# Handing dt·u·B from TensorE to VectorE by PSUM banks in a four-layer scan kernel

## The chip, the cores and the metric

The kernel runs on one core of a Trainium2 chip, as one program for all four layers. The metric is the device time of one execution in microseconds. Engines are called by the profile's names: PE (TensorE, the matmuls), PEld (its weight loads), DVE (VectorE), ACT (ScalarE), POOL (GpSimd), SP (the queue that issues most DMAs).

## What is computed

A picture of 4 x 64 x 64 positions and 192 channels goes through four layers, each with a group norm ahead of it and a residual sum behind it. Layers 0 and 3 scan every image in four directions (rows, columns, and both backwards); layer 1 does the same with sequences of only 64 positions, one per line; layer 2 is a Toeplitz product and has no scan. The change concerns the selective scan that layers 0, 1 and 3 share. Cut to its core, for every channel and each of 16 states:

```python
def step(h, inp):
    u_l, dt_l, Bl, Cl = inp
    dA = jnp.exp(dt_l[..., None] * A[None])
    h = dA * h + (dt_l * u_l)[..., None] * Bl[:, :, None, :]
    y = jnp.sum(h * Cl[:, :, None, :], axis=-1)
    return (h, y)
```

In layers 0 and 3 the state `h` runs through all 4096 positions of an image; in layer 1 it starts at zero on every line of 64.

## The kernel before

**Jobs and units.** The sequence is cut into chunks of 512 positions (`T`). One chunk in one direction is a *job*: 128 jobs in each of layers 0, 1 and 3. A job is cut into *units*: 64 channels times 4 of the 16 states. The 128 partitions hold the 64 channels twice (`q` = 0, 1), each half with two states along the free dimension, so a unit is a tile of 128 x 1024. Layers 0 and 1 have 384 inner channels and 24 units per job, layer 3 has 192 and 12.

**One unit, engine by engine.**
- PE makes `b` = dt·u·B in PSUM (`feed`, line 378): the transposed dt·u of 64 channels is the loaded weight, a diagonal matrix of B values (`diag`) is what streams. A unit takes 4 position blocks of 128 (`k`) times 2 halves (`q`), 8 products of 256 columns. An fp32 product shows as two MATMUL records, so a fill of `b` is 16 records.
- ACT makes dA = exp(dt·A) by two instructions of 512 elements (line 401), into one of three SBUF tiles.
- DVE runs the recurrence (`scan`): in layers 0 and 3 one scan of 512 per state, with a carry from the chunk before (line 418); in layer 1 a single scan of 1024 (line 411), since dA is zero at the start of each line.
- POOL multiplies by C (line 422), and PE sums the two partition halves and the states into `y` (`collect`, line 447, four records of 512 columns per unit).

**Direct units.** In part of the units (pair `p` = 3; one of two channel groups in layer 0, both in layers 1 and 3: 3 of 24, 6 of 24, 3 of 12 units per job) PE has no part in `b`. POOL makes it in SBUF (`spread`, line 351), and dA goes into the PSUM tile that `b` would have had.

**Layout of `b`.** The PSUM tile is 128 x 1024 fp32, two banks of 512, and there are two such tiles (pool `b`, 2 buffers). In layers 0 and 3 the states alternate element by element (`(l n)`): block `k` fills 256 neighbouring elements, blocks 0 and 1 the first bank, 2 and 3 the second, and either state's scan reads every second element of both banks. In layer 1 the tile is `(h n l)`: the first half of the positions with both states is the first bank, the second half the second.

**What sets the order.** The whole program is unrolled. `run_jobs` walks over the units; at unit i it issues `feed` of unit i+2, `scan` of unit i, `spread` of unit i+3, `collect` of a finished pair, and then the preparatory steps that are due there by hand-set offsets (`when`: projections, softplus in `finish`, line 271, the product dt·u, line 278, transposes `turn`, line 285, step sizes, line 259) and the loads that `plan` places. Each engine works through its own instructions in that order. Waits are placed by the framework from the regions that instructions read and write. dt·u is made by DVE in layer 0 and 3 (line 278) and by POOL in layer 1.

**Around the scans.** Each image of layers 0 and 3 also has an input stage (norm, projection, convolution) and an output stage; they are not touched.

Of the kernel before, what the change touches and what calls it, by code (L numbers as in the profile page):

```python
# [9 lines left out]
ALU = mybir.AluOpType  # L10
# [9 lines left out]
T = 512  # L20
# [3 lines left out]
NB = T // 128  # L24
# [12 lines left out]
class Kernel:  # L37
# [316 lines left out]
    def feed(self, job, t, p, c, pools):  # L354

        nc = self.nc
        w, rev, g = job["w"], job["rev"], 2 * t + c
        lines = job["carry"] is None
        direct = c in job["direct"].get(p, ())
        wide = pools["b"].tile([128, 2 * T], F32, name="b")  # L360
        if direct:
            b = job["bs"].pop((t, p, c))
        else:
            b = wide
        for k in range(0 if direct else NB):
            for q in range(2):
                half = b[q * 64 : (q + 1) * 64, :]
                if lines:
                    to = half.rearrange("p (h n l) -> p h n l", h=2, n=2)
                    off = k % 2 * 128  # L370
                    to = to[:, k // 2, :, off : off + 128]
                else:
                    to = half[:, k * 256 : (k + 1) * 256].rearrange("p (l n) -> p n l", n=2)
                if isinstance(job["dtuT"], dict):
                    dtu = job["dtuT"][t][:, k, c * 64 : (c + 1) * 64]
                else:
                    dtu = job["dtuT"][:, k, g * 64 : (g + 1) * 64]
                nc.tensor.matmul(  # L378
                    to, dtu, job["diag"][p][:, k, 2 * q : 2 * q + 2, :],
                    start=True, stop=True,  # L380
                )
        delta = job["both"][g]
        if lines:
            if job.get("begin"):
                job.pop("begin")()
            if direct:
                dA = wide
                at = HW - 1 if rev else 0
                nc.scalar.copy(dA[:, at::HW], job["zero"])
            else:  # L390
                self.turns_dA += 1
                dA = job["dA"][self.turns_dA % len(job["dA"])]
            inner = slice(0, HW - 1) if rev else slice(1, HW)
            of = delta.rearrange("p (h a b) -> p h a b", h=2, b=HW)[:, :, :, inner]
            to = dA.rearrange("p (h n a b) -> p h n a b", h=2, n=2, b=HW)[:, :, :, :, inner]
            to = [to[:, :, n] for n in range(2)]
        else:
            of, dA = delta, wide if direct else pools["work"].tile([128, 2 * T], F32, name="dA", bufs=3)
            to = [dA[:, n * T : (n + 1) * T] for n in range(2)]
        for n in range(2):  # L400
            nc.scalar.activation(to[n], of, AF.Exp, scale=w["A"][:, g, 2 * p + n : 2 * p + n + 1])  # L401
        job["fed"][t, p, c] = b, dA, direct

    def scan(self, job, t, p, c, pools):
        nc = self.nc
        rev, carry, g = job["rev"], job["carry"], 2 * t + c
        way = slice(None, None, -1) if rev else slice(None)
        b, dA, direct = job["fed"].pop((t, p, c))
        h = pools["work"].tile([128, 2 * T], F32, name="h", bufs=7 if carry is None else 4)
        if carry is None:  # L410
            nc.vector.tensor_tensor_scan(h[:, way], dA[:, way], b[:, way], 0.0, ALU.mult, ALU.add)  # L411
        else:
            by_n = b.rearrange("p (n l) -> p n l" if direct else "p (l n) -> p n l", n=2)
            dA = dA.rearrange("p (n l) -> p n l", n=2)
            hn = h.rearrange("p (n l) -> p n l", n=2)
            for n in range(2):
                start = 0.0 if job["first"] else carry[g, p][:, n : n + 1]
                nc.vector.tensor_tensor_scan(  # L418
                    hn[:, n, way], dA[:, n, way], by_n[:, n, way], start, ALU.mult, ALU.add
                )  # L420
        hc = h if carry is None else pools["work"].tile([128, 2 * T], F32, name="hc", bufs=5)
        nc.gpsimd.tensor_mul(hc, h, job["cbc"][p])  # L422
        job["done"][t, p, c] = hc
        if carry is None:
            return None

        def after():
            nc.scalar.copy(carry[g, p], hn[:, :, 0 if rev else T - 1])

        return after  # L430
# [799 lines left out]
```

## Time and profile before

| what | value |
|---|---|
| median of 3 runs | 30885.05 us (30880.78 to 30885.68) |
| the profiled execution: its own time | 30865.86 us |
| its span, first to last instruction | 30864.0 us, mean granted PE clock 0.961 |
| busy share of the span: PE, DVE, ACT, POOL | 87%, 72%, 75%, 74% |
| layer 0, scans of one image (32 jobs) | about 2285 us, four times |
| layer 1, all scans (128 jobs) | 10905 us |
| layer 3, scans of one image (32 jobs) | about 1234 us, four times |

The three scan stages were found from the first and the last of POOL's products by C. Divided by their jobs they give 71.4, 85.2 and 38.6 us per job. The shares of the page are means over stages with different limits, so the three stages have to be read apart. A group line of the page reads: line of the kernel, engine, operation, tile written and tiles read, shape, count; then busy us and mean ns of one; then the idle time just before these instructions and what ended it. A timeline line reads: start and length in us, engine, line, operation, count of merged instructions, and in brackets the idle time before it and what ended it. Matmul records overlap: their spacing from start to start is what PE needs, not their length.

### The profile page before, as it was taken

To read this page: it belongs to the slowest core of one execution; us is meant where nothing else is said; L and a number is where in the kernel's file an instruction comes from. 1 tells how busy PE (TensorE), PEld (TensorE's weight loads), DVE (VectorE), ACT (ScalarE), POOL (GpSimd) and SP (SyncE) were. 2 spreads that over 40 slices of the span, in tenths; PEclk is the share of its full clock that TensorE was granted. 3 is DMA by queue.
4 is the path that set the end of the run, shared out by engine and by line. 5 is a ranking of instruction groups with operands and counts; after the bars stand their busy time and mean duration, and the time that the engine had idled before them with its cause. 6 is when DMAs were issued, how large, how long until landed. Compare 5 with 4: busy or idle time off the path is not lost. (4 is left out here: it accounts for less than half of the span.)

```text
span 30864.0 us, 503255 instructions
## 1 busy us (share of the span) xinstructions
PE 26878.4 (87%) x189464; PEld 15827.7 (51%) x189464; DVE 22327.6 (72%) x16587; ACT 23000.6 (75%) x50177; POOL 22890.6 (74%) x9831
## 2 busy tenths in 40 slices
PE   8998998999899688888888888888588988888888
PEld 5664665666466444444444444444355444444444
DVE  7887888788788777777777777777423267777777
ACT  7885886788588588888888888888232278788888
POOL 7885885888588499989998999999100077777777
PEclk9999999999999899999999999999788999999999
DMA  3334333433433533333333333333533345545454
GB/s 109 100 99 117 101 98 104 112 100 99 119 101 97 142 99 97 97 100 101 101 104 97 98 97 99 102 101 102 131 78 76 104 131 131 132 130 134 128 135 128
DMA packets 1652695, 3342.38 MB, mean 108 GB/s; under 512 B 396725, under 2 KB 453494, under 8 KB 1634646
## 3 DMA queue, kind: packets, MB, share of 16 engines
q1 hardware_dynamic: 1541718, 3142.34, 38.1%
q10 hardware_dynamic: 108544, 167.85, 1.6%
q8 instruction: 1497, 24.53, 0.4%
q14 instruction: 936, 7.67, 0.1%
HBM read 2149.81 MB, written 656.08 MB: 91 GB/s over the span
## 5 line engine op out<-in xcount | busy, mean ns | idle before, releaser
L378 PE MATMUL b<-diag,dtuT 128*64 128x256 f32 x98304 | 12607.9, 386 | 1732.9 <-DVE h L411 917.9
L422 POOL TENSOR_TENSOR hc<-h,c 128x1024 f32<-128x1024 f32 x4608 | 10943.4, 2395 | 1515.0 <-DVE h L418 1158.3
L378 PEld LDWEIGHTS b<-diag,dtuT 128*64 128x64 f32 x98304 | 8214.9, 138 | 6212.3 <-DVE h L411 1903.3
L401 ACT ACTIVATE dA<-both,A 128x512 f32<-128x512 f32 (+1 forms) x12288 | 8267.7, 711 | 2124.3 <-DVE h L411 1472.0
L418 DVE TENSOR_TENSOR_SCAN h<-dA,carry,b 128x512 f32<-128x512 f32 x6720 | 8169.8, 1263 | 1367.8 <-PE b L378 861.4
L422 POOL TENSOR_TENSOR h<-h,c 128x1024 f32<-128x1024 f32 x3072 | 7219.1, 2374 | 1049.2 <-DVE h L411 880.3
L332 ACT ACTIVATE diag<-ident,bt 128x128 f32<-128x128 f32 x20480 | 6570.6, 391 | 92.2 <-issue 91.4
L447 PE MATMUL y<-hc,fold 128*64 128x512 f32 x18432 | 5783.3, 599 | 386.1 <-POOL hc L422 384.4
L411 DVE TENSOR_TENSOR_SCAN h<-dA,b 128x1024 f32<-128x1024 f32 x2304 | 5202.8, 2274 | 1147.3 <-ACT dA L401 798.4
L351 POOL TENSOR_TENSOR bs<-dtu,bc 128x1024 f32<-128x1024 f32 x1536 | 3639.4, 2369 | 158.5 <-DMA c<-bc_dram 72.8
L447 PE MATMUL y<-h,fold 128*64 128x512 f32 x12288 | 3259.6, 593 | 10.2 <-POOL h L422 10.2
L501 POOL MEMSET pad<- 128x13068 f32 (+1 forms) x8 | 73.4, 9172 | 3968.3 <-DMA inw<-in_L_in_w 2997.7
L411 DVE TENSOR_TENSOR_SCAN h<-b,bs 128x1024 f32<-128x1024 f32 x768 | 1758.9, 2290 | 1413.6 <-ACT b L401 1102.8
L447 PEld LDWEIGHTS y<-hc,fold 128*64 128x64 f32 x18432 | 1924.0, 138 | 1550.1 <-POOL hc L422 813.1
L401 ACT ACTIVATE b<-both,A 128x504 f32<-128x504 f32 (+1 forms) x3072 | 2076.2, 676 | 376.4 <-DVE h L418 328.3
L418 DVE TENSOR_TENSOR_SCAN h<-b,carry,bs 128x512 f32<-128x512 f32 x1344 | 1639.2, 1260 | 220.9 <-issue 170.4
L237 PEld LDWEIGHTS dtu_ps<-ident,dtu 128*64 128x64 f32 (+1 forms) x16384 | 1183.2, 141 | 497.6 <-issue 375.9
L447 PEld LDWEIGHTS y<-h,fold 128*64 128x64 f32 x12288 | 1005.0, 137 | 795.2 <-issue 444.9
L418 DVE TENSOR_TENSOR_SCAN h<-dA,b 128x512 f32<-128x512 f32 x960 | 1112.8, 1205 | 352.8 <-PE b L378 191.3
L401 ACT ACT_TABLE_LOAD x1019 | 1307.4, 1283 | 11.8
L237 PE MATMUL dtu_ps<-ident,dtu 128*64 128x128 f32 (+1 forms) x16384 | 1272.7, 273 | 45.9 <-DVE dtu L278 41.5
L827 DVE SCALAR_TENSOR_TENSOR u<-in_ps,conv_w,u 128x504 f32<-128x504 f32 (+2 forms) x1152 | 831.6, 722 | 411.7 <-ACT u L822 402.6
(157 smaller groups left out, 24601.4 us busy)
## 6 DMA issues: line engine op xcount, KB each, us to landing
c<-bc_dram SPq DMA_DIRECT2D x3072, 256.0 KB, 4.1
both<-delta SPq DMA_DIRECT2D x2048, 128.0 KB, 2.7
bc<-bc_dram SPq DMA_DIRECT2D x768, 256.0 KB, 4.2
both<-delta_dram SPq DMA_DIRECT2D x1536, 128.0 KB, 3.7
dtu<-dtu_dram SPq DMA_DIRECT2D x1536, 128.0 KB, 2.7
dtu<-dtu SPq DMA_DIRECT2D x1280, 128.0 KB, 2.5
L_y<-out ACTq DMA_DIRECT2D x512, 256.0 KB, 3.0
u<-L_u SPq DMA_DIRECT2D x160, 768.0 KB, 5.4
```

The costliest lines, as they stand in the source:

```text
L237: nc.tensor.matmul(to[half * 64 : (half + 1) * 64], of[:, half * 64 : (half + 1) * 64], self.ident[:p, :p], start=True, stop=True,)
L332: nc.scalar.activation(to, self.ident, AF.Copy, scale=of)
L351: self.nc.gpsimd.tensor_mul(by(b), dtu, by(job["bbc"][p]))
L378: nc.tensor.matmul(to, dtu, job["diag"][p][:, k, 2 * q : 2 * q + 2, :], start=True, stop=True,)
L401: nc.scalar.activation(to[n], of, AF.Exp, scale=w["A"][:, g, 2 * p + n : 2 * p + n + 1])
L411: nc.vector.tensor_tensor_scan(h[:, way], dA[:, way], b[:, way], 0.0, ALU.mult, ALU.add)
L418: nc.vector.tensor_tensor_scan(hn[:, n, way], dA[:, n, way], by_n[:, n, way], start, ALU.mult, ALU.add)
L422: nc.gpsimd.tensor_mul(hc, h, job["cbc"][p])
L447: nc.tensor.matmul(y[c * 64 : (c + 1) * 64, :], self.fold, of, start=first == 0 and n == 0, stop=last == LAST and n == 1)
L501: nc.gpsimd.memset(pad, 0.0)
L827: nc.vector.scalar_tensor_tensor(u[:, :, to], ps[:, :, of], tap(3 - j), u[:, :, to], ALU.mult, ALU.add)
```

## The change

In layers 0 and 3 each state gets one bank of the PSUM tile: the products are cut from 256 to 128 columns, all of state 0 first (blocks 0 to 3, both halves), then all of state 1. A fill is then 16 products, 32 records, in place of 8 and 16, and the scan of a state reads one bank, element after element. In layer 1 the products stay as they are, but backward directions make blocks 2 and 3 before 0 and 1, and the scan of 1024 is cut into two scans of 512, each over one bank, both with the start value 0.0; in backward directions the upper one runs first.

```diff
+        turns = []
+        if lines and not direct:
+            turns = [(k, slice(0, 2)) for k in ((2, 3, 0, 1) if rev else range(NB))]
+        elif not direct:
+            turns = [(k, slice(n, n + 1)) for n in range(2) for k in range(NB)]
+        for k, n in turns:
-        for k in range(0 if direct else NB):
             for q in range(2):
                 half = b[q * 64 : (q + 1) * 64, :]
                 if lines:
...
                 else:
-                    to = half[:, k * 256 : (k + 1) * 256].rearrange("p (l n) -> p n l", n=2)
+                    off = n.start * T + k * 128
+                    to = half[:, off : off + 128]
...
-                nc.tensor.matmul(
-                    to, dtu, job["diag"][p][:, k, 2 * q : 2 * q + 2, :],
-                    start=True, stop=True,
-                )
+                of = job["diag"][p][:, k, 2 * q + n.start : 2 * q + n.stop, :]
+                if not lines:
+                    of = of[:, 0, :]
+                nc.tensor.matmul(to, dtu, of, start=True, stop=True)
...
         if carry is None:
-            nc.vector.tensor_tensor_scan(h[:, way], dA[:, way], b[:, way], 0.0, ALU.mult, ALU.add)
+            for at in (T, 0) if rev else (0, T):
+                one = slice(at, at + T)
+                nc.vector.tensor_tensor_scan(
+                    h[:, one][:, way], dA[:, one][:, way], b[:, one][:, way], 0.0, ALU.mult, ALU.add
+                )
         else:
-            by_n = b.rearrange("p (n l) -> p n l" if direct else "p (l n) -> p n l", n=2)
+            by_n = b.rearrange("p (n l) -> p n l", n=2)
```

`lines` and `carry is None` mean layer 1; `direct` units have no products. Nothing else changes.

## The prediction

> **What bounds the kernel now.** I read the page's groups first, then the busy time of each engine in the scan stages (image 0 of layer 0, all of layer 1, image 0 of layer 3), then the timeline of single jobs.
>
> ```profile
> L378 PE MATMUL b<-diag,dtuT 128*64 128x256 f32 x98304 | 12607.9, 386 | 1732.9 <-DVE h L411 917.9
> L418 DVE TENSOR_TENSOR_SCAN h<-dA,carry,b 128x512 f32<-128x512 f32 x6720 | 8169.8, 1263 | 1367.8 <-PE b L378 861.4
> L411 DVE TENSOR_TENSOR_SCAN h<-dA,b 128x1024 f32<-128x1024 f32 x2304 | 5202.8, 2274 | 1147.3 <-ACT dA L401 798.4
> ```
>
> ```profile
> core 0: us, PE busy (x) PEld busy (x) DVE busy (x) ACT busy (x) POOL busy (x), PEclk, DMA share, GB/s
> 190.00:2475.00 2285.00, 2135.26 (x16612) 1487.15 (x16608) 1955.75 (x1612) 1897.95 (x4702) 2021.31 (x863) 0.97 0.38 97
> 10811.00:21716.00 10905.00, 9711.19 (x69924) 5058.93 (x69922) 7956.07 (x4717) 9104.84 (x16955) 9856.90 (x4358) 1.00 0.35 99
> 24875.00:26109.00 1234.00, 1085.58 (x8120) 651.97 (x8120) 987.65 (x828) 1169.91 (x2996) 1149.70 (x480) 1.00 0.52 135
> ```
>
> Three limits: in layer 0 PE is busy 93% of the stage, in layer 1 POOL 90%, in layer 3 ACT 95%. In layer 0 DVE often waits for a fill of `b`:
>
> ```profile
> DVE h L418 <- PE b L378: 223.0, 251, 2.2
> ```
>
> That is 7.0 us in each of the 32 jobs. One job, PE and then ACT:
>
> ```profile
> 1502.50 1.93 PE L378 MATMUL b<-diag,dtuT 128*64 128x256 f32 x16
> 1504.22 1.06 PE L447 MATMUL y<-hc,fold 128*64 128x512 f32 x4
> 1505.08 1.93 PE L378 MATMUL b<-diag,dtuT 128*64 128x256 f32 x16
> ...
> 1516.01 3.68 PE L378 MATMUL b<-diag,dtuT 128*64 128x256 f32 x16 [3.87 <-DVE h L418]
> ```
>
> ```profile
> 1526.60 1.34 ACT L401 ACTIVATE dA<-both,A 128x512 f32<-128x512 f32 x2 [2.38 <-DVE h L418]
> 1529.21 0.72 ACT L401 ACTIVATE dA<-both,A 128x512 f32<-128x512 f32 x1 [1.19 <-DVE h L418]
> ```
>
> PE runs without a hole except once a job: DVE waits for softplus and makes dt·u (1508.33, 2.82 us), both PSUM tiles stay full, PE stands 3.87 us and restarts cold. So a job of layer 0 is a loop: PE fills (1516 to 1529), DVE's scans end, ACT gets its dA tiles back (1529.21) and is then nearly gapless until the next job's softplus, dt·u, two units of scans, PE.
>
> [...] a scan that reads both banks starts only after a fill's last record, 0.14 us behind it. [...] with every second element written a fill goes from first to last start in 1.93 - 0.38 = 1.55 us, in layer 1 with runs of 128 in 1.95 - 0.38 = 1.57. I book no gain for the contiguous write. [...]
>
> **The change part by part.**
>
> *Products of 128 columns.* The fill takes 1504.22 - 1502.50 = 1.72 us, 16 records at 108 ns[...]. The transposes have the shape that comes (64 weights, 128 columns):
>
> ```profile
> 2023.26 0.71 PE L237 MATMUL dtu_ps<-ident,dtu 128*64 128x128 f32 x9
> 22326.89 21.44 PE L1080 MATMUL yt_ps<-xt,mat 64*64 64x64 f32 x384 [0.57 <-ACT xt L1073]
> ```
>
> (0.71 - 0.27) / 8 = 55 ns from start to start, with a weight load for each; layer 2 holds (21.44 - 0.28) / 383 = 55.2 ns over 384 records. So 32 records take 1.74 to 1.77 us; I take +0.03 us a fill (ends +0.01 and +0.05).
>
> *The handoff.* A wait goes by the region read, a tile's reuse by the whole tile:
>
> ```profile
> 2032.21 2.45 DVE L418 TENSOR_TENSOR_SCAN h<-dA,carry,b 128x512 f32<-128x512 f32 x2 [1.01 <-PE b L378]
> 2032.33 0.72 ACT L401 ACTIVATE dA<-both,A 128x512 f32<-128x512 f32 x1
> ```
>
> The first scan starts before ACT has begun the second half of its dA, so it will also start on bank 0 while PE fills bank 1. But ACT at 1526.60 starts when both scans of the tile's last user are over (1524.11 + 2.45), though the first had freed its half 1.2 us before. So PE doesn't get a tile back sooner; only DVE gets it earlier, by half a fill, 0.86 us, plus 0.11 because the last record lasts 273 ns in place of 386. The first scan (1.20 us) covers the rest of the fill, so the pair ends 0.97 us earlier wherever DVE was waiting for PE, as at 1526.73.
>
> *Layer 0 on its chain.* ACT's wait ending at 1529.21 shortens by 0.97. Behind it ACT has 0.1 and 0.8 us of slack left until softplus; I carry 0.9 us to dt·u and to PE's restart. The three fills between restart and 1529 cost 3 x 0.03 = 0.1. In jobs where softplus hangs on PE more directly, 21 fills cost 0.6, of which a PE wait on DVE of 0.5 (at 2136.83) absorbs most. Net -0.85 us a job, x 128 = **-109 us**; ends -0.6 and -1.1: -77 to -140. Hidden: DVE's other 6 us of waits per job. They are PE's own pace (a unit with a transpose needs 1.73 + 0.86 + 0.87 = 3.46 us of PE), and an earlier start of a scan doesn't speed that.
>
> *Layer 1.* Two scans for one:
>
> ```profile
> 26411.32 4.55 DVE L418 TENSOR_TENSOR_SCAN h<-dA,b 128x512 f32<-128x512 f32 x4 [9.51 <-DMA dtu<-dtu]
> 14999.81 4.46 DVE L411 TENSOR_TENSOR_SCAN h<-dA,b 128x1024 f32<-128x1024 f32 x2
> ```
>
> 4.55 against 4.46 us: +0.05 us a unit, on all 3072 (154 us of DVE time, mostly hidden: DVE is busy 73%). A job's chain goes POOL's `bs` (15032.0), two scans, ACT, one scan, ACT gapless, one scan, ACT, one scan (15082.30), POOL: five scans, +0.25 us, x 128 = **+32 us** (0 to +70). The earlier start wins nothing there: these scans wait for ACT or POOL, and each exp writes both banks of a direct tile. ACT, queued behind a scan for its dA tile, is in the five.
>
> *Layer 3.* ACT is the limit; its waits (0.93 and 0.68 us a job at 27328.16 and 27329.51) hang on a projection behind PE's fill, not on the handoff: 2 x 0.03 x 128 = **+6 us** (-30 to +20).
>
> Sum: -109 + 32 + 6 = -71 us on 30865.86 gives 30795; the median lies 19 us above the profiled run: **30814 us**.
>
> **Rivals.**
> - *PE pays for the split (slower).* If a weight load (138 ns) no longer hides behind a product half as long, each record costs more. Layer 0 is PE-bound, so 21 fills a job pay: at 58 ns a record a fill is 1.86 us, 21 x 0.13 - 1.4 = +1.3 us a job, +166, and with +38 from the other layers 31090. It decides from about 55.7 ns: 21 x 0.052 us equals the gain less those 38 us. For it: that is only 0.5 ns above the 384-record run, and PEld is already busy 65% in layer 0. Against it: both bursts hold 55 ns with a load for every record.
> - *The handoff isn't on the path.* If ACT's own queue paces softplus, layer 0 stays, the rest costs 38: 30923. That the scan waited for the whole tile after all gives the same time. Against it: the 1.19 us wait at 1529.21.
> - *The hole shrinks too.* PE's stop is 3.87 to 4.48 us. The cold fill spreads its starts over 2.8 us in place of 1.6, and the transposes behind it lose as much. If half of the 128 jobs stay warm, 64 x 2.4 = 154 us more: 30660. Against it: both ends of the hole move together.
>
> **How the numbers follow.** Forecast 0.55, slower PE 0.18, no path 0.14, warm restart 0.13. About 0.2%, 62 us, is what a measurement of this kernel can tell from no change. The forecast's own ends are 30740 to 30880; I put 0.35 of its 0.55 below 30823 and 0.20 within. With the warm restart faster is 0.48; same 0.20 + 0.08 = 0.28; slower 0.18 + 0.06 = 0.24. The range 30620 to 31000 leaves out the dearer half of the first rival and a little below.
>
> **What would show it.** Right: L378 records in layer 0 at 54 to 56 ns from start to start; DVE's wait for `b` there well below 223 us an image; its scan starting under half a fill after the first record; 70.5 us a job in layer 0, 85.5 in layer 1, 38.6 in layer 3. Wrong: records above 56 ns, a PE fill that starts before both scans of the tile's last user end, or a layer 3 that moves by over 0.3 us a job.

## The result, and the profile after

The changed kernel takes 31288.92 us (median of 4 runs, 31284.16 to 31294.73), the kernel before, in the same session, 30885.36 (30880.78 to 30887.13): ratio 1.0132, 95% interval 1.012 to 1.0144. It is 404 us slower, outside the stated range of 30620 to 31000. The profiled execution spans 31292.9 us, 428.9 more than that of before.

The groups of the page; the lines of the kernel have moved (378 is now 387, 401 is 407, 411 is 419, 418 is 428, 422 is 432, 447 is 457), and move again in the kernels of the experiments:

```profile
L387 PE MATMUL b<-diag,dtuT 128*64 128x128 f32 (+1 forms) x159744 | 12804.9, 304 | 2043.6 <-DVE h L419 1124.9
...
L428 DVE TENSOR_TENSOR_SCAN h<-dA,carry,b 128x512 f32<-128x512 f32 x6720 | 8179.3, 1264 | 1406.2 <-PE b L387 951.4
...
L419 DVE TENSOR_TENSOR_SCAN h<-dA,b 128x512 f32<-128x512 f32 x4608 | 5351.4, 1204 | 1285.2 <-ACT dA L407 846.1
```

PE has more records (159744 against 98304) for nearly the same busy time (12804.9 us against 12607.9), DVE's scans of layers 0 and 3 cost what they did (1264 ns against 1263), and layer 1's cost more: 149 us in the units that PE fills (5351.4 against 5202.8), 47 in the direct ones (1805.9 against 1758.9). And DVE's idle time ended by PE's `b` has grown from 861.4 to 951.4, where the forecast wanted it to shrink. The busy time of the engines in image 0 of layer 0, in layer 1 and in image 0 of layer 3 (columns as in the prediction's table):

```profile
190.00:2480.00 2290.00, 2118.60 (x27116) 1660.59 (x27114) 1940.78 (x1598) 1898.81 (x4689) 2001.43 (x854) 0.97 0.37 98
10850.00:21950.00 11100.00, 9892.98 (x69966) 5882.37 (x69968) 8070.04 (x7786) 9169.48 (x17011) 9829.55 (x4348) 0.98 0.34 98
25152.00:26426.00 1274.00, 1104.84 (x12696) 797.99 (x12696) 990.73 (x829) 1176.11 (x2997) 1149.89 (x480) 0.98 0.49 131
```

No engine does much more than before (the largest rise is PE's in layer 1, 9892.98 us against 9711.19); all three stages are longer. From POOL's first to its last product by C, layer 0 takes 2310.5 us an image (2282.9 before, means of four), layer 1 11062.8 (10904.6), layer 3 1273.4 (1233.9): +110, +158 and +158 us, together 427 of the 429 us between the two traces.

**The handoff isn't split.** DVE's waits for a fill in image 0 of layer 0 rose from 223.0 us (us in total, number of waits, longest):

```profile
DVE h L428 <- PE b L387: 259.2, 367, 3.8
```

PE and DVE in one job of that image:

```profile
1520.95 1.92 PE L387 MATMUL b<-diag,dtuT 128*64 128x128 f32 x32
1522.70 1.03 PE L457 MATMUL y<-hc,fold 128*64 128x512 f32 x4
...
1523.02 2.45 DVE L428 TENSOR_TENSOR_SCAN h<-dA,carry,b 128x512 f32<-128x512 f32 x2 [1.02 <-PE b L387]
```

The fill's last record ends at 1520.95 + 1.92 = 1522.87, and the pair of scans starts at 1523.02: 0.15 us behind the whole tile, as before, and not behind the half that the first scan reads. It is so throughout: of the 2688 fills of layer 0, the 2304 of layer 1 and the 1152 of layer 3 none has a scan that starts before the fill's last record has ended.

**Where the time goes.** POOL takes each unit's product in a fixed order, so the mean idle time ahead of the product of unit 0, 1, 2 ... of a job shows where a job got longer. The means here and below leave out the first and the last job of an image (of 32 jobs in layer 1). Most of the 24 (12) units moved by under 0.06 us; those that moved most, mean us a job:

| layer, unit | before | after |
|---|---|---|
| 0, unit 5 (direct) | 0.02 | 0.62 |
| 1, unit 17 | 0.00 | 1.05 |
| 1, unit 18 | 1.26 | 0.52 |
| 1, unit 20 | 0.00 | 0.21 |
| 1, unit 21 (direct) | 0.00 | 0.54 |
| 3, unit 5 (direct) | 0.00 | 0.90 |
| 3, unit 9 (direct) | 1.58 | 2.24 |

**What stands there in the traces.** The engines don't issue their instructions as the program text has them: the framework lays out each engine's order, and after the change it laid it out anew. Of the 50177 places in ScalarE's sequence 9002 hold another operation than before, of GpSimd's 9831 none. In layer 0 TensorE's sequence changed as well, VectorE's did not; in layers 1 and 3 VectorE's changed too, in layer 3 in 28 places. In layer 0, ACT around unit 5, before:

```profile
483.68 0.58 ACT L616 COPY out<-y 128x512 f32<-128x512 f32 x1
...
484.15 0.73 ACT L401 ACTIVATE dA<-both,A 128x512 f32<-128x512 f32 x1
...
484.78 0.68 ACT L401 ACTIVATE b<-both,A 128x512 f32<-128x512 f32 x1
...
485.39 0.71 ACT L401 ACTIVATE dA<-both,A 128x512 f32<-128x512 f32 x1
...
486.00 0.68 ACT L401 ACTIVATE b<-both,A 128x512 f32<-128x512 f32 x1
...
486.78 2.46 DVE L418 TENSOR_TENSOR_SCAN h<-b,carry,bs 128x512 f32<-128x512 f32 x2 [0.20 <-ACT b L401]
```

and after, in the same job:

```profile
489.02 1.35 ACT L407 ACTIVATE dA<-both,A 128x512 f32<-128x512 f32 x2
...
490.26 0.59 ACT L626 COPY out<-y 128x512 f32<-128x512 f32 x1
...
490.73 0.43 ACT L332 ACTIVATE diag<-ident,bt 128x128 f32<-128x128 f32 x1
...
491.27 0.69 ACT L407 ACTIVATE b<-both,A 128x512 f32<-128x512 f32 x1
...
491.98 0.72 ACT L407 ACTIVATE dA<-both,A 128x512 f32<-128x512 f32 x1
...
492.61 0.67 ACT L407 ACTIVATE b<-both,A 128x512 f32<-128x512 f32 x1
...
493.38 2.46 DVE L428 TENSOR_TENSOR_SCAN h<-b,carry,bs 128x512 f32<-128x512 f32 x2 [1.34 <-ACT b L407]
```

The direct unit's two exps (written to a `b` tile) now stand behind both of another unit's dA, a copy and a diagonal; DVE waits 1.34 us for the second in place of 0.20. In layer 3's backward jobs, PE and DVE before:

```profile
26895.96 1.03 PE L447 MATMUL y<-hc,fold 128*64 128x512 f32 x4
26896.82 0.59 PE L625 MATMUL fold_ps<-out,fold 128*64 128x512 f32 x1
...
26899.26 0.66 DVE L614 TENSOR_TENSOR out<-fold_ps,earlier 64x512 f32<-64x512 f32 x1
```

and after:

```profile
27215.99 1.03 PE L457 MATMUL y<-hc,fold 128*64 128x512 f32 x4
27220.32 1.08 PE L457 MATMUL y<-hc,fold 128*64 128x512 f32 x4 [3.29 <-POOL hc L432]
27221.23 0.59 PE L635 MATMUL fold_ps<-out,fold 128*64 128x512 f32 x1
...
27222.29 0.68 DVE L624 TENSOR_TENSOR out<-fold_ps,earlier 64x512 f32<-64x512 f32 x1 [3.52 <-PE fold_ps L635]
27222.90 2.44 DVE L428 TENSOR_TENSOR_SCAN h<-b,carry,bs 128x512 f32<-128x512 f32 x2
```

The fold product (it adds the two partition halves of a finished `out`), for which everything was there, now stands on PE behind a `y` product that waits 3.29 us for POOL. DVE stands in front of `out` for 3.52 us, and the scan that POOL needs next is queued behind it. In layer 1, DVE after:

```profile
11836.71 1.21 DVE L419 TENSOR_TENSOR_SCAN h<-dA,b 128x512 f32<-128x512 f32 x1
11837.84 0.71 DVE L837 SCALAR_TENSOR_TENSOR u<-in_ps,conv_w,u 128x496 f32<-128x496 f32 x1
11838.46 1.21 DVE L419 TENSOR_TENSOR_SCAN h<-dA,b 128x512 f32<-128x512 f32 x1
11839.59 0.70 DVE L837 SCALAR_TENSOR_TENSOR u<-in_ps,conv_w,u 128x488 f32<-128x488 f32 x1
```

With two half scans to a unit, an operation of the convolution (a *tap*, line 837) can be set between the halves, and POOL, which needs both, waits for it (0.88 us ahead of its product at 11839.82). This is so in 378 units, three a job.

### The profile page after: what moved, and what is told of

The parts are those of the page before. It is cut to its first block, busy times and chain, and to the rows that moved or that the text cites. A ratio compares the mean times of both kernels' runs of the same rounds, so it can differ in the third digit from the quotient of the medians.

```text
span 31292.9 us, 634272 instructions
## 1 busy us (share of the span) xinstructions
PE 27122.6 (87%) x250904; PEld 17972.8 (57%) x250904; DVE 22478.4 (72%) x19659; ACT 23095.9 (74%) x50177; POOL 22899.0 (73%) x9831
## 5 line engine op out<-in xcount | busy, mean ns | idle before, releaser
L387 PE MATMUL b<-diag,dtuT 128*64 128x128 f32 (+1 forms) x159744 | 12804.9, 304 | 2043.6 <-DVE h L419 1124.9
L387 PEld LDWEIGHTS b<-diag,dtuT 128*64 128x64 f32 x159744 | 10529.2, 139 | 5249.9 <-issue 2708.9
L428 DVE TENSOR_TENSOR_SCAN h<-dA,carry,b 128x512 f32<-128x512 f32 x6720 | 8179.3, 1264 | 1406.2 <-PE b L387 951.4
L419 DVE TENSOR_TENSOR_SCAN h<-dA,b 128x512 f32<-128x512 f32 x4608 | 5351.4, 1204 | 1285.2 <-ACT dA L407 846.1
L457 PE MATMUL y<-hc,fold 128*64 128x512 f32 x18432 | 5431.2, 602 | 510.2 <-POOL hc L432 510.0
L457 PE MATMUL y<-h,fold 128*64 128x512 f32 x12288 | 3560.8, 609 | 8.9 <-POOL h L432 8.9
L419 DVE TENSOR_TENSOR_SCAN h<-b,bs 128x512 f32<-128x512 f32 x1536 | 1805.9, 1211 | 1269.3 <-POOL h L432 515.5
L457 PEld LDWEIGHTS y<-hc,fold 128*64 128x64 f32 x18432 | 1556.0, 138 | 1351.8 <-POOL hc L432 924.3
L457 PEld LDWEIGHTS y<-h,fold 128*64 128x64 f32 x12288 | 1180.7, 142 | 716.5 <-issue 490.3
L428 DVE TENSOR_TENSOR_SCAN h<-dA,b 128x512 f32<-128x512 f32 x960 | 1111.5, 1205 | 374.9 <-PE b L387 204.5
```

The costliest lines, as they stand in the source:

```text
L387: nc.tensor.matmul(to, dtu, of, start=True, stop=True)
L419: nc.vector.tensor_tensor_scan(h[:, one][:, way], dA[:, one][:, way], b[:, one][:, way], 0.0, ALU.mult, ALU.add)
L428: nc.vector.tensor_tensor_scan(hn[:, n, way], dA[:, n, way], by_n[:, n, way], start, ALU.mult, ALU.add)
L457: nc.tensor.matmul(y[c * 64 : (c + 1) * 64, :], self.fold, of, start=first == 0 and n == 0, stop=last == LAST and n == 1)
```

## The experiments

Kernel 1 is the kernel of experiment 1, and so on. Theory O: the loss is the new order of instructions. Theory P: it is the operations themselves, twice the products in layers 0 and 3 and twice the scans in layer 1. To tell them apart, an engine's order is *tied*: the program is laid out once in the version whose order is wanted, and in the version that runs the instructions of each engine are chained in that order. The chain fixes the order of issue and is declared without a wait (`NoSync`); where a fill or scan has another number of instructions, the group stands where the other's stood. In the traces of kernels 1 to 3 the sequences of ScalarE, VectorE and GpSimd agree with those wanted in every place (a unit's two half scans counted as one).

```diff
+    nc = make(NEW, BANKS, make(LIKE, LIKE_BANKS))
...
+            tc.add_manual_dep(i, last[e].name, free, reason="order")
```

**1. New operations, old order** (NEW: layers 0, 1, 3; LIKE: the kernel before; all engines).

> All operations are those of the changed kernel; only the order in which each engine (TensorE, VectorE, ScalarE, GpSimd, SyncE) issues them is tied to that of the kernel before (a fill of 32 products stands where the fill of 16 stood, the two half scans of layer 1 stand together where the one scan stood). Theory O (the loss is the new order of instructions that the scheduler chose when the operations changed): layer 0 back to about 2283 us an image, layer 3 to 1234, layer 1 to 10905 to 10940 (five scans a job on the chain by 0.05 us: at most +32), in all 30,870 to 30,940, ratio 0.9995 to 1.002. Theory P (the loss is the operations themselves: twice the products, twice the scans, more semaphore signals): about 31,290 as the changed kernel, ratio 1.013.

Measured: 30931.22 us, ratio 1.0021 (1.0013 to 1.0029). Layer 0 2288.7 us an image, layer 1 10944.0, layer 3 1234.5. The idle time of units 5 in layers 0 and 3 is gone (0.02 and 0.00 us), and layer 1's extra 39 us are in units 18 and 0, ahead of which POOL already waited. This is what theory O said: the operations alone make 64 us, against the 30867.61 that the kernel before took in the same session.

**2. Old operations, new order** (NEW: none; LIKE: the changed kernel).

> The reverse: all operations are those of the kernel before, 256-column products and one scan a unit in layer 1; each engine issues them in the order of the changed kernel (a fill or a scan stands where the last part of its group stood). Theory O: the loss comes without the change, layer 0 about 2310 us an image, layer 3 about 1273, layer 1 11,020 to 11,070, in all 31,220 to 31,300, ratio 1.011 to 1.0135. Theory P: 30,885 within 0.2%, ratio 1.000.

Measured: 30850.61 us, ratio 0.9995 (0.9986 to 1.0004): the total fits theory P, and the layers show that this is chance. Layer 3 takes 1272.5 us an image, all of the changed kernel's loss without one changed operation. Layer 0 takes 2287.2, only +4. Layer 1 takes 10711.7, which is 193 *less* than before. So O holds in layer 3, and in layer 1 the new order is good as long as a scan is one instruction. In layer 0 the two don't add: order alone +17 us over four images, operations alone +23, both +110. The 0.6 us ahead of unit 5 come with the order (0.59 here), but with the old operations the job wins 0.41 back ahead of unit 15 (0.29 against 0.70), with the new ones nothing (0.74).

**3. A real handoff by banks, old order.** As 1, and in layers 0 and 3 each bank is a tile of its own.

```diff
+            wide = [pools["b"].tile([128, T], F32, name="b", bufs=4) for n in range(2)]
...
+                    to = b[n.start][rows, k * 128 : (k + 1) * 128]
```

> As the first kernel of this call (new operations in the old order), and in layers 0 and 3 the two PSUM banks of a unit are two tiles of their own instead of one tile of two banks, so the first scan waits for the 16 records of its own bank only, and a bank is filled again as soon as its own scan is over. This makes the handoff that the forecast assumed. If the forecast's layer 0 step holds once the handoff is really split: layer 0 by 20 to 35 us an image below the first kernel (2250 to 2263), layer 3 within 3 us of it, in all 30,760 to 30,840. If the handoff is not on the path (the second rival): layer 0 within 8 us an image of the first kernel, in all within 30 us of it.

Measured: 30581.15 us, ratio 0.9907 (0.9892 to 0.9922), more than expected. Layer 0 takes 2186.9 us an image, 102 less than kernel 1; layer 3 1248.7, 14 more. DVE's waits for `b` in image 0 of layer 0:

```profile
DVE h L446 <- PE b L401: 150.0, 258, 1.8
```

It was 237.4 in kernel 1. One fill, on the timeline:

```profile
1608.95 1.63 PE L401 MATMUL b<-diag,dtuT 128*64 128x128 f32 x26
1610.37 0.59 PE L475 MATMUL y<-hc,fold 128*64 128x512 f32 x1
1610.42 0.49 PE L401 MATMUL b<-diag,dtuT 128*64 128x128 f32 x3
...
1610.18 3.88 DVE L446 TENSOR_TENSOR_SCAN h<-dA,carry,b 128x512 f32<-128x512 f32 x3 [0.59 <-PE b L401]
```

The scan starts at 1610.18; the fill's last three records, which run beside the first `y` product, end at 1610.42 + 0.49 = 1610.91. With a tile to a bank the scan starts 0.73 us ahead of the fill's end, and not 0.15 behind it; in layer 0 this is so, by more or less, in 2219 of 2688 fills. In layer 3 POOL waits 2.04 us ahead of unit 1 (0.47 before).

**4. The same with a free order** (layers 0 and 3 new with two tiles, layer 1 as before, nothing tied).

> Layers 0 and 3 with one state to a bank and the two banks as two tiles; layer 1 with the operations of before; the order is left to the scheduler. In layer 1 it keeps the order of before, in layers 0 and 3 it chooses a new one. Theory O: layer 1 10,905 within 10 us, layers 0 and 3 move by their order as well as by the split, by anything from -35 to +40 us an image and not by what the first three kernels show for the operations. Theory P: layer 0 +26 and layer 3 +39 us an image as in the changed kernel, less what the split handoff gives, layer 1 as before.

Measured: 30883.89 us, ratio 1.0007 (0.9998 to 1.0015). Layer 1 10904.6, as before; layer 0 2229.0 us an image, 42 more than in the tied order, with 0.32 us ahead of unit 5 again; layer 3 1291.4, 43 more than tied, with 0.97 ahead of unit 5. Against the kernel before, layer 0 wins 54 us an image in this order and layer 3 loses 57.5: in sum nothing is left of the gain.

**5. The halves of layer 1 together.** The changed kernel tied to its own order, but the two half scans stand where the second stood.

```diff
+            if of == 2 and WHOLE:
+                one = one if at == 1 else []
+            elif of:
+                one = one[at * n // of : (at + 1) * n // of]
```

> The changed kernel in its own order, but for layer 1's two half scans of a unit: they stand together, where the second stood, so VectorE's tap operations that the changed kernel issues between two halves are issued before both. Theory Q (layer 1 loses by the work that stands between the halves): 10,711 (one scan a unit in this order) + 39 (what two scans cost in the old order) = 10,750, in all 30,960 to 31,000. Theory R (two scans cost more in this order wherever the taps stand): layer 1 at 11,063 within 40 us, in all about 31,290. Layers 0 and 3 stay at 2310 and 1273 us an image under both.

Measured: 30963.54 us, ratio 1.003 (1.0019 to 1.0042). Layer 1 takes 10759.7, 303 less than in the changed kernel. DVE:

```profile
11789.09 2.32 DVE L439 TENSOR_TENSOR_SCAN h<-dA,b 128x512 f32<-128x512 f32 x2
11791.33 0.70 DVE L859 SCALAR_TENSOR_TENSOR u<-in_ps,conv_w,u 128x488 f32<-128x488 f32 x1
11791.95 2.33 DVE L439 TENSOR_TENSOR_SCAN h<-b,bs 128x512 f32<-128x512 f32 x2
```

Theory Q holds: what layer 1 lost is the work between the halves. The second scan of a unit itself costs 10759.7 - 10711.7 = 48 us in this order, 39 in the old one. Layer 0, which has the changed kernel's order on every engine, takes 2304.1 us an image here and 2310.5 there, so differences of up to 6 us an image in layer 0, such as those of kernels 1 and 2 against the kernel before, stand for little.

**6. One engine tied in each layer** (ScalarE in layer 0, VectorE in layer 1, TensorE in layer 3, each to the order of before).

> The changed kernel's operations; tied to the order of the kernel before are ScalarE alone in layer 0, VectorE alone in layer 1, TensorE alone in layer 3, all else is free. If the traces are read rightly (layer 0: ScalarE brings the direct unit's exps too late; layer 1: VectorE's taps stand between the halves; layer 3: TensorE has the fold product behind the y product that waits for GpSimd): layer 0 2289 us an image, layer 1 10,944, layer 3 1235, each within 6 us an image (25 in layer 1), in all 30,900 to 30,970. A layer whose loss sits in another engine's order stays at 2310, 11,063 or 1273.

Measured: 31192.35 us, ratio 1.0105 (1.009 to 1.012). Layer 0: 2299.8 us an image where 2289 was expected, a miss; the wait ahead of unit 5 is 0.02, as read, but units 10 and 15 wait 0.16 and 0.17 us longer than in the kernel before. By the traces, this layer differs from kernel 1 in TensorE's order alone (11 us an image) and from the changed kernel in ScalarE's (11 us; of SyncE's transfers 16 stand elsewhere too): about half of the order's cost is either's. Layer 3: 1216.3 where 1235 was expected, with no wait ahead of unit 5. TensorE's new order was what the loss hung on: with it tied, the framework gave VectorE its old order back by itself, so what VectorE's 28 places cost isn't told apart. ScalarE and GpSimd have an order here that neither kernel had, and with it the layer takes 18 us an image less than in kernel 1. Layer 1: 11233.3, a miss. VectorE's order alone, with the others free, is worse than either: 4.39 us ahead of unit 0. An engine's order is good only together with that of the others.

**7. The bank refilled only after both scans.** As 3, with one more wait, the one that a shared tile would have.

```diff
+            at = job["at", t, p, c] + 2
+            if banks and at < len(self.wides):
+                self.tc.add_manual_dep(self.wides[at].ins, one.ins.name, wait, reason="both scans")
```

> As the kernel with two tiles of one bank in the old order (30,581), but a unit's first bank is refilled only when both scans of the unit that had it are over, as with one tile of two banks. What is left is the step of the forecast alone: the first scan starts half a fill earlier. Forecast: layer 0 by 27 us an image below the 2289 of the new operations in the old order, 2262. If the gain of that kernel came from the earlier refill instead: 2280 to 2289. If the earlier start of the scan is all of it: 2187. In layer 3 the 15 us an image that the two tiles lost go if the earlier refill made them.

Measured: 30781.4 us, ratio 0.9972 (0.9961 to 0.9983). Layer 0 takes 2236.7 us an image: 52 less than kernel 1, where the forecast's step said 27, and the earlier refill gives another 50 (kernel 3). The traces show the same: in kernel 3 a unit's first fill record or exp stands before the second scan of the bank's last user in 451 of 3070 cases, among them units 13 and 14 of every job, in kernel 7 in none.

Layer 3 stays at 1251.2, so the refill isn't what costs there. The traces of kernels 1 and 3 show what does, here in the fourth job of image 0 (kernel 1, then kernel 3):

```profile
25067.75 7.97 POOL L450 TENSOR_TENSOR hc<-h,c 128x1024 f32<-128x1024 f32 x3
25071.63 1.88 DVE L279 TENSOR_TENSOR dtu<-delta,u 96x1024 f32<-96x1024 f32 x1 [0.71 <-ACT delta L272]
```

```profile
24665.84 6.99 POOL L450 TENSOR_TENSOR hc<-h,c 128x1024 f32<-128x1024 f32 x3
24670.67 3.24 DVE L279 TENSOR_TENSOR dtu<-delta,u 96x1024 f32<-96x1024 f32 x1 [1.04 <-ACT delta L272]
24676.42 2.36 POOL L450 TENSOR_TENSOR hc<-h,c 128x1024 f32<-128x1024 f32 x1 [3.59 <-DVE h L446]
```

Where VectorE's product dt·u meets a product of GpSimd, it ends 1.08 us behind the end of one (121 of layer 3's 128 jobs in kernel 1, 124 in kernel 3); where it meets none it takes 1.22 us. With two tiles it comes earlier in GpSimd's product, stands 3.24 us in place of 1.88, and the scans behind it come too late for unit 1. In the 71 jobs of kernel 3 in which dt·u takes over 3 us, unit 1 waits 3.25 us, in 49 others 0.28.

**8. The best of each layer.** Layer 0 as in 3; layer 1 with one scan a unit, in the changed kernel's order; the rest as before.

> Layer 0 with one state to a bank in two tiles of one bank, in the order of the kernel before; layer 1 with the operations of the kernel before (one scan a unit) in the order of the changed kernel; layers 2 and 3 as the kernel before. If the layers add up as the first call measured them (layer 0 -384 us in all, layer 1 -193, layer 3 0): layer 0 2184 to 2190 us an image, layer 1 10,705 to 10,720, layer 3 1234, in all 30,270 to 30,330. If the gain of layer 1 came from the order outside layer 1: layer 1 10,905 and 30,480.

Measured: 30294.13 us, ratio 0.9813 (0.9799 to 0.9828), layer 0 2184.5, layer 1 10711.1, layer 3 1233.5. The layers add up.

**9. Layer 0 alone, nothing tied.**

> No order is tied anywhere. Layer 0 alone is changed: one state to a bank, the two banks as two tiles of one bank. Layers 1 and 3 have the operations of the kernel before, and the scheduler gives them the order of before. Theory O: layer 0 as in the kernel with two tiles and a free order (2223 to 2237 us an image, some 50 more than in the tied order, since the scheduler picks another order for ScalarE), layer 1 10,905 and layer 3 1234 as before, in all 30,630 to 30,680. If layer 0's order were of no account: 2187 us an image and 30,480.

Measured: 30665.32 us, ratio 0.9934 (0.9919 to 0.9949); 2230.7, 10906.4 and 1233.4. This is the version that needs only a change of source.

**10. Layer 3 added.**

> As the kernel put together from the best of each layer (30,294), and layer 3 as in the kernel with one engine tied in a layer: 128-column products, TensorE in the order of before, the other engines free. If the layers add up: layer 3 1216 us an image in place of 1234, in all 30,210 to 30,240. If layer 3's 1216 depended on what ran before it: 1234 and 30,294.

Measured: 30217.6 us, ratio 0.979 (0.9775 to 0.9804), the fastest: 2186.3, 10714.6 and 1214.5. Of its page, and of its windows image 0 of layer 0:

```profile
L450 DVE TENSOR_TENSOR_SCAN h<-dA,carry,b 128x512 f32<-128x512 f32 x6720 | 8139.8, 1262 | 1046.0 <-PE b L405 597.5
```

```profile
190.00:2380.00 2190.00, 2104.66 (x27334) 1798.82 (x27331) 1949.33 (x1612) 1900.08 (x4704) 2016.64 (x863) 0.99 0.39 102
```

DVE's idle time behind PE's `b` is 597.5 us, from 861.4 before, and PE is busy 96% of layer 0's stage, from 93%.

**11. Two tiles in layer 1 too.** As 10, with two half scans together and a tile to a bank in layer 1; a direct unit's two exps become four.

> As the kernel before this one in the call, but layer 1 with two half scans of a unit, which stand together, in the order of the changed kernel, and with two tiles of one bank: the first half scan waits for its own bank only, and a direct unit's two exps become four of half the size. The forecast said that the earlier start wins nothing in layer 1, since the scans on its chain wait for ScalarE or GpSimd: then layer 1 stays at the 10,760 of the halves that stand together in one tile, up to 10,850 if ScalarE's four more starts a direct unit are on the path, in all 30,260 to 30,370. If the handoff by banks counts in layer 1 as it did in layer 0 (1.6 us a job and more): layer 1 at 10,560 or below, in all under 30,080.

Measured: 30348.95 us, ratio 0.9832 (0.9815 to 0.9848); layer 1 10840.4, inside what the forecast's reading gave. The handoff by banks has nothing to win that would show in layer 1: the stage is 81 us longer than in kernel 5, though DVE's waits for a fill fell there from 192 us to 1. ScalarE has 2304 instructions more (exps and the zeros at the start of a line), and is busy 9435.34 us of 10800 there, against 9043.97 of 10600 in kernel 10. That this is the price is an estimate: no run has these instructions without the second tile.

## Why the prediction was wrong

**Products of 128 columns: right.** From the fill's first record to the next product it was 1.72 us and is 1522.70 - 1520.95 = 1.75, the +0.03 of the forecast (medians of all fills that a `y` product follows: 1.73 and 1.75). The records of a median fill stand 54 ns apart, before 103 to 105. The first rival, in which PE pays 58 ns and the kernel takes 31090, landed nearest, but its mechanism isn't there.

**The handoff: the step that failed first.** That a scan "will also start on bank 0 while PE fills bank 1" was concluded from ACT's dA, a tile in SBUF. The line shown for it doesn't show it: the scan at 2032.21 reads a dA made from 2024.82 to 2026.16, and the exp at 2032.33 belongs to a later unit, whose scan starts at 2038.25. Of dA it is true all the same: in the trace of before 335 of layer 0's 2688 first scans start before the second exp of their own dA has ended. What failed is the step from there to a tile in PSUM. There the wait is for the whole tile, and not only when PE writes it: in the direct units ACT writes dA into that tile by two instructions, and none of layer 0's 384 first scans starts before the second has ended, before or after the change; with a tile to a bank and a free order (kernel 9) 198 do. So the sentence that waits are placed by the regions read and written holds here for the tile in SBUF and not for the one in PSUM; why the framework tells them apart isn't shown. The scan 0.14 us behind a fill in the prediction doesn't tell the one from the other: that scan needed both banks. The whole-tile wait was named inside the second rival ("that the scan waited for the whole tile after all"), with 30923 us, 38 more than before. Kernel 1, which has these operations in the order the forecast had in mind, takes 64 more: 23 in layer 0, where the rival has none (the changed kernel and kernel 5, with one order, differ there by 26), 39 in layer 1 and 3 in layer 3. The second rival was close to right on the operations.

**The size of the handoff.** Made real, the step is worth 4 x 52 = 208 us in layer 0 (kernel 7 against kernel 1), 1.6 us a job, where the forecast carried 0.9 before the price of the products. It followed one chain, from a scan to softplus, and called DVE's other waits PE's own pace, hidden. They weren't: POOL's idle time ahead of units 15 to 19 fell as well (together 3.29 us a job before, 2.15 in kernel 7, 0.63 in kernel 3). And reuse by the bank, which it excluded for one tile, gives as much again.

**Layers 1 and 3, the operations: right.** Two scans cost 2 x 5351.4 / 4608 - 5202.8 / 2304 = 0.06 us a unit more (0.05 forecast); on the path +39 us (forecast +32). Layer 3 moved by +3 in the old order (forecast +6, though 2 x 0.03 x 128 is 8), and of layer 1's earlier start no gain is seen (kernel 11).

**What the sum left out: the order.** All its terms stood on the order of before; that one could be another was in none of them. The description of the kernel even says that each engine works in the order of the program text, which the traces contradict. The order makes some 340 us of the 404 (404 less kernel 1's 64; the stages of the traces of the changed kernel and of kernel 1 differ by 362): in layer 3 the fold product behind a waiting `y` product (+154 with no changed operation, gone with TensorE tied), in layer 1 the taps between half scans (303 us, against an order that would else have won 193), in layer 0 the direct unit's exps too late, and TensorE's new order, which shows at unit 15. POOL's wait there is under 0.7 us in some jobs and 0.8 to 1.9 in others, before, after and in kernels 1 and 2 (in kernel 3 it is gone). In these four traces a wait of over 0.9 us comes only in jobs in which PE restarts slowly after its hole (see the third rival), but not in all of these. What else decides, and so why order and operations don't add in layer 0, stays open. The sign to look for was there in the forecast's own list, "a layer 3 that moves by over 0.3 us a job" (it moved by 1.2): it said that something else was at work, not what.

**The third rival** (the hole shrinks) calls the fill behind the hole cold: 3.68 us at 1516.01, at a granted clock of 0.50 from 1516.00 to 1519.70, where a fill takes 1.93 us at 1.00 from 1502.00 to 1507.00. That a shorter hole spares PE this was its author's estimate. The hole didn't shrink in the changed kernel: in image 0 of layer 0 there are 31 fills behind a hole of over 2 us, before and after, and the median hole grew from 4.20 to 4.67 us. But something of the rival did come. In all of layer 0, PE's records behind the hole last 634 ns in place of 379 (421 in place of 273 at 128 columns) in 109 of 123 such fills before and 103 of 124 after, and in only 67 of 120 in kernel 1, 70 of 124 in kernel 7 and 43 of 117 in kernel 3, whose median hole in image 0 is 2.62 us. So the slow restarts that the rival hoped to save do get fewer in these kernels; what share of layer 0's times hangs on them no run tells. In kernel 3 one follows 35 of the 68 holes of 2 to 3 us, so the length of the hole alone doesn't decide. (The slow fill that the rival reads spreads its starts over 3.04 us, not 2.8.)

## What to carry to other kernels

Where a framework lays out the engines' order, a change of the number or size of instructions is also a change of order: compare the sequences of both kernels, engine by engine, before explaining a time, and tie the order to price the operations. A handoff by PSUM banks needed a tile to a bank here (in kernel 3 2219 of layer 0's 2688 units then had a scan start ahead of the fill's end); a split inside one tile moved nothing (none of 6144 did in the changed kernel). An instruction cut in two gives the scheduler a place to put other work between the halves (in 378 units here, 303 us of layer 1), so cut only where somebody can use the first half. And where one engine takes units in a fixed order, its idle time unit by unit finds the few places at which a loss sits.

## What was not expected of the hardware

The price of the order itself: with the same operations layer 3 takes 1216.3 us an image in kernel 6, 1234.5 in kernel 1 and 1273.4 in the changed kernel, a spread of 5%, by the order of the instructions alone. VectorE's product dt·u in layer 3, which takes 1.22 us when it meets no product of GpSimd, ended 1.08 us behind one in 123 of the 124 jobs of the kernel before in which it met any (in kernels 1 and 3 as told above), and so took up to 3.00 us before, 3.35 in the changed kernel and 3.24 in the job of kernel 3 shown above, by the moment at which it came; GpSimd's next product, when it met the same dt·u, took 3.33 us in place of 2.37. In these traces the two products behave as if they could not run at the same time, while VectorE's scans run beside GpSimd's products: of the 6720 of line 418 in the kernel before that read a dA in SBUF and a carry, 2744 lie wholly within a product of GpSimd and take 1265 ns, and the 223 that meet none take 1257. And records of 128 columns start 54 ns apart, where those of 256 start 103 to 105 ns apart, with a weight load for each: PE pays 0.02 us a fill (1.75 us against 1.73) for halving its products here.
